# Values of layers 0 and 2 by one level of Strassen's algorithm, with the token sums of queries and keys

## Chip, cores and metric

The kernel runs on one core of one Trainium2 chip. The metric is the device time of one execution in microseconds (us). Three runs of the kernel before took 3003.57, 3005.7 and 3009.11 us; the median is 3005.7. The profile is of one more execution, of 3005.96 us, with a span of 3004.2 us from the first to the last instruction and a granted TensorE clock of 0.99.

## The reference

The input x has 128 graphs of 64 tokens with 512 features, in float32, and each graph has a boolean adjacency matrix. Four layers follow one another; each adds something to x. Before each layer the rows are normalized and negative values set to zero:

```python
h = jnp.maximum(_layernorm(x, axis=-1), 0.0)
x = x + _L0_gnn_ref(h, adj, Wq, Wk, Wv, Wo, bo)
```

Layers 0 and 2 are attention of 4 heads of 64, so Wq, Wk and Wv are 512 by 256 and Wo is 256 by 512:

```python
q = split_heads(x @ Wq); k = split_heads(x @ Wk); v = split_heads(x @ Wv)
sim = jnp.where(adjacency_mask, q @ k.T * scale, neg)
out = softmax(sim) @ v
return out @ Wo + bo
```

Layers 1 and 3 are wider forms of the same (8 heads) and are not touched by the change. Everything is float32.

## The kernel before

**Steps.** The 8192 token rows are cut into 16 blocks of 512 tokens. A step is one block in one layer: 16 steps to a layer, 64 in all, of which 32 belong to layers 0 and 2. A step loads its rows in two halves (L468, tile xin), normalizes them (DVE L433 to L442 for the statistics, with a power on POOL at L440, then ACT L449), transposes them on TensorE (L500, tile ptr; ACT copies them to the tile hT at L505), projects them to queries, keys and values, forms scores (L847, tile sc), does the softmax (DVE L858, L863, L866, L872 and L874, ACT L869, POOL L876, tile E), transposes it (L887, tile ptp), multiplies it by the values (L1006, tile po), projects by Wo and adds the residual (tile xres, loaded at L927, with the bias added by POOL at L931, stored at L972).

**Strassen products.** Queries and keys together (weights w_qk), the projection by Wo, and all projections of layers 1 and 3 are done by `winograd`: the weights A and the tokens B are split two by two, and seven products are formed instead of eight. The sums that this needs are made once for the weights (POOL, `sums_of_a`, L315), and in every step for the tokens (`sums_of_b`, tile t: by POOL at L327 from hT, by DVE at L324 from the attention's output m). A tile of weights has seven slots; a product is called here by its slot: A0, A1, A5, A4, A2, A6, A3, in the order in which they run. A0, A5, A2 and A3 go to one PSUM bank (mA), A1 to another (mB), A4 and A6 to a third (mC). A product that goes on in a bank waits for the copy of what the bank held to be read (`read` in the code): ACT copies at L552 and L572, or to the tile u at L947 for Wo, whose copies POOL adds to xres at L952. DVE adds the others (L565, L576).

**Values of layers 0 and 2.** These are done directly, by `v_proj` (L682): for each of 4 blocks of 128 tokens, 4 matmuls of 128 by 128 tokens against 256 columns of Wv, into one of the two banks that mB and mC also use (tile mmv), and one ACT copy (`evict`, L674). A float32 matmul stands in the trace as two records, called passes here.

**Order.** Nothing is scheduled by hand. Seven streams (weights, loads, layernorms, transposes, projections, fronts for scores and softmax, attentions) are Python generators; each yields what it will do next, with an assumed duration (`pe(0.432)`, `act(0.6)`) or an event to wait for. `Order.run` always takes the stream that can start earliest by these assumed times, then the one of the lower priority number, and writes its instruction. So the assumed durations settle the fixed order of instructions on each engine. [...] The SP queue issues the loads and stores of xin and xres, in order; the loads of weights go out from ACT's queue.

**Buffers that matter.** xin: 4 halves; xres: 2 halves; t: 3; hT: 2; V: 2; PSUM banks: 2 for mA, 2 shared by mB, mC, mmv and mmf, 2 for ptr and ptp, 2 for sc and po.

Of the kernel before, what the change touches and what calls it, by code (L numbers as in the profile page):

```python
# [14 lines left out]
P = 128  # L15
D = 512
N = 64
TB = 4
NC = D // P
# [163 lines left out]
def pe(us):  # L183
    return ("pe", us, 0.25)


def dve(us):
    return ("dve", us, 0.1)


def act(us):
    return ("act", us, 0.1)


def pool(us):
    return ("pool", us, 0.15)
# [7 lines left out]
def gnn_stack(ctx: ExitStack, tc: tile.TileContext, a: dict, out: bass.AP):  # L204
# [80 lines left out]

    def v_part(t):

        return t.rearrange("p a k n -> p (a k) n")[:, 0:4]

    def o_part(t):  # L290

        return t.rearrange("p a k n -> p (a k) n")[:, 4:11, None, :]

    def wo_halves(t, n):
        v = o_part(t)[:, 0:4, 0].rearrange("p (i j) n -> p i j n", i=2)
        return [(a[n][:, i * H:(i + 1) * H], v[:, i]) for i in range(2)]

    units = [("qk0", lambda t: halves(t, "Wq0", "Wk0")),
             ("vo0", lambda t: [(a["Wv0"], v_part(t))] + wo_halves(t, "Wo0")),
             ("q1", lambda t: halves(t, "Wq1")), ("k1", lambda t: halves(t, "Wk1")),  # L300
             ("v1", lambda t: halves(t, "Wv1")), ("o1", lambda t: halves(t, "Wo1")),
             ("qk2", lambda t: halves(t, "Wq2", "Wk2")),
             ("vo2", lambda t: [(a["Wv2"], v_part(t))] + wo_halves(t, "Wo2")),
             ("map3", lambda t: halves(t, "map3")), ("sem3", lambda t: []),
             ("q3", lambda t: halves(t, "q3")), ("k3", lambda t: halves(t, "k3"))]
    for key, _ in units:
        w_ready[key], w_sums[key] = od.event(), od.event()
    bo, bo_done = {}, {}

    def sums_of_a(A):  # L310

        for o, i0, i1, op in ((4, 2, 3, ALU.add), (5, 4, 0, ALU.subtract),
                              (6, 1, 5, ALU.subtract), (2, 0, 2, ALU.subtract)):
            yield pool(1.3)
            nc.gpsimd.tensor_tensor(A[:, o], A[:, i0], A[:, i1], op)  # L315

    def sums_of_b(B, T, vector=False):
# [11 lines left out]
    def weights():  # L329
        for key, parts in units:  # L330
            if key == "q1":
                yield p_ready[0, 0]
            t, w_done[key] = yield from r_w.new(f"w_{key}")
            W[key] = t
            for src, dst in parts(t):
                yield ("actq", 1.0, 10.0)
                nc.scalar.dma_start(dst, src.rearrange("(c p) o -> p c o", p=P))
            if key in ("vo0", "o1", "vo2"):
                l = int(key[-1])
                src = a[f"bo{l}"]  # L340
                bo[l], bo_done[l] = yield from r_u.new(f"bo{l}")
                yield ("actq", 0.5, 2.0)
                nc.scalar.dma_start(bo[l], bass.AP(tensor=src.tensor, offset=src.offset,
                                                   ap=[[0, P], [1, D]]))
            if key in ("q1", "k1", "v1"):
                yield from gamma_into(key)
            elif key == "o1":
                yield from v_bias()
            elif key == "sem3":
                yield from gcn_fold(t)  # L350
            w_ready[key].set()
            yield from sums_of_a(o_part(t) if key in ("vo0", "vo2") else t)
            w_sums[key].set()

    bv = const.tile([P, NC], F32, name="bv")
# [171 lines left out]

    def product(bank, A, B, tokens_out, first):

        KC = A.shape[1]  # L530
        for m in range(2):
            o = bank[:, m * H:(m + 1) * H]
            for k in range(KC):
                yield pe(0.432)
                if tokens_out:
                    l, r = B[:, k, m * P:(m + 1) * P], A[:, k, :]
                else:
                    l, r = A[:, k, m * P:(m + 1) * P], B[:, k, :]
                nc.tensor.matmul(o, l, r, start=(first and m == 0 and k == 0),  # L539
                                 stop=(k == KC - 1), skip_group_check=True)  # L540

    class Out:

# [4 lines left out]
        def first(self, i, k, p_, read, done):  # L548
            o, p3 = self.view(i, k), both(p_)
            if self.bias is None:  # L550
                yield act(0.6)
                nc.scalar.copy(o, p3)  # L552
            else:
                for m in range(2):
                    yield act(0.45)
                    nc.scalar.activation(o[:, m], p3[:, m], AF.Identity,  # L556
                                         bias=self.bias[:, 2 * i + m:2 * i + m + 1])
            read.set()
            done.set()

        def second(self, i, k, p_, after, done):
            yield after
            o = self.view(i, k)
            yield dve(0.69)
            nc.vector.tensor_add(o, both(p_), o)  # L565
            done.set()

        def add(self, i, k, p_, after, read, done):

            o, t = self.view(i, k), self.view(i, 1 - k)  # L570
            yield act(0.6)
            nc.scalar.copy(t, both(p_))  # L572
            read.set()
            yield after
            yield dve(0.7)
            nc.vector.tensor_add(o, o, t)  # L576
            done.set()

# [3 lines left out]
    def winograd(A, BT, tokens_out, out_, used, begun):  # L582

        B, T, *sums = BT

        def ev(n):
            return [od.event() for _ in range(n)]

        def first(i, k, p_):
            read, done = ev(2)  # L590
            od.spawn(out_.first(i, k, p_, read, done), 0)
            return read, done

        def second(i, k, p_, after):
            done = od.event()
            od.spawn(out_.second(i, k, p_, after, done), 0)
            return done

        def add(i, k, p_, after):
            read, done = ev(2)  # L600
            od.spawn(out_.add(i, k, p_, after, read, done), 0)
            return read, done

        p_, pe_ = yield from r_ma.new("mA")
        yield from product(p_, A[:, 0], B(0, 0), tokens_out, True)
        read, c11 = first(0, 0, p_)
        q_, qe = yield from r_mm.new("mB")
        yield from product(q_, A[:, 1], B(1, 0), tokens_out, True)
        c11 = second(0, 0, q_, c11)
        od.spawn(when([c11], qe), 0)  # L610
        yield read
        for e in sums:
            yield e
        yield from product(p_, A[:, 5], T[:, 1], tokens_out, False)
        read, u2 = first(0, 1, p_)
        r_, re_ = yield from r_mm.new("mC")
        yield from product(r_, A[:, 4], T[:, 0], tokens_out, True)
        read5, c22 = first(1, 1, r_)
        yield read
        yield from product(p_, A[:, 2], T[:, 2], tokens_out, False)  # L620
        read, c22 = add(1, 1, p_, c22)
        begun.set()
        yield read5
        yield from product(r_, A[:, 6], B(1, 1), tokens_out, False)
        c12 = second(0, 1, r_, u2)
        od.spawn(when([c12], re_), 0)
        yield read
        yield from product(p_, A[:, 3], T[:, 3], tokens_out, False)
        od.spawn(out_.alone(1, 0, p_, pe_), 0)
        od.spawn(when([c11, c12, c22, pe_], used), 0)  # L630
# [38 lines left out]
        yield begun  # L669
        return used  # L670

    def evict(o, p_, e):
        yield act(0.4)
        nc.scalar.copy(o, p_)  # L674
        e.set()

    def v_proj(inT, w, t):
        n = w.shape[2]
        p_, e = yield from r_mm.new("mmv")
        for c in range(NC):  # L680
            yield pe(0.857 * n / 512)
            nc.tensor.matmul(p_[:, 0:n], inT[:, c, t * P:(t + 1) * P], w[:, c, :],  # L682
                             start=(c == 0), stop=(c == NC - 1))
        return p_[:, 0:n], e

    st, p_ready, s_ready, p_used, with_ones = {}, {}, {}, {}, []

    def projections(steps):
        for l, s in steps:
# [4 lines left out]
            if l in (0, 2):  # L694
                yield w_ready[f"qk{l}"]
                qk, z["qk_done"] = yield from r_qk.new("qk")
                used = yield from unit(W[f"qk{l}"], (*BT, w_sums[f"qk{l}"]), False, Out(quarters(qk)))
                od.spawn(when([used], s_ready[l, s], t_done[l, s],
                              w_done[f"qk{l}"] if end else None), 0)
                z["q"], z["k"] = qk[:, 0:2, :], qk[:, 2:4, :]  # L700
                yield w_ready[f"vo{l}"]
                V, z["v_done"] = yield from r_v.new("V")
                es = [used]
                for t in range(TB):
                    p_, e = yield from v_proj(h, v_part(W[f"vo{l}"]), t)
                    od.spawn(evict(V[:, t, 0:D // 2], p_, e), 0)
                    es.append(e)
                z["v"] = V
                od.spawn(when(es, p_ready[l, s], h_done[l, s]), 0)
            elif l == 1:  # L710
                es = []
                for i, n in enumerate("qk"):
# [510 lines left out]
```

## Time and profile before

| | us busy | share of the span |
|---|---|---|
| TensorE, matmuls (PE) | 2938.9 | 98% |
| TensorE, weight loads (PEld) | 2493.5 | 83% |
| POOL | 1493.8 | 50% |
| DVE | 1744.9 | 58% |
| ACT | 1358.7 | 45% |

Layer 0 takes the stretch from 14.5 us to about 520, layer 2 that from 1437.8 to about 1950; in between and after lie layers 1 and 3. In the stretches 119.8 to 491.5 and 1522.2 to 1921.4 the steps repeat one pattern. The page's groups give, for each kind of instruction, the busy time, the mean of one in ns and, after the second bar, how long its engine stood idle just before and for whom. The timeline gives start, duration, engine, line and operation of merged neighbours, in order of time; "x16" means sixteen records, and the idle time before is in brackets. Matmul records overlap: each is the time from its start to its end, and the next starts sooner.

### The profile page before, as it was taken

The page shows a single profiled execution, that of the slowest core. Times are in us where ns is not written, and L with a number is a line of the kernel's source. Part 1 is how long each engine was busy: PE and PEld are TensorE (multiplying, and loading weights), DVE is VectorE, ACT ScalarE, POOL GpSimd, SP SyncE. Part 2 cuts the span into 40 slices and gives each one's busy share as a digit, 9 for nine tenths or more (in the row PEclk, how much of TensorE's full clock was granted, in tenths as well). Part 3 has the DMA queues.
Part 4 walks back from the last instruction along what each step waited for, and adds up shares of the span by engine and source line. Part 5 has one row for each costly group of instructions (what it writes and reads, how often), then busy time and mean ns, then how long its engine had stood idle before and what let it go on. Part 6 is the DMA issues. An engine that isn't in the chain of part 4 may idle for free.

```text
span 3004.2 us, 64290 instructions
## 1 busy us (share of the span) xinstructions
PE 2938.9 (98%) x27288; PEld 2493.5 (83%) x27288; DVE 1744.9 (58%) x2753; ACT 1358.7 (45%) x2489; POOL 1493.8 (50%) x1168
## 2 busy tenths in 40 slices
PE   8999999999999999999999999999999999999997
PEld 7888888888888888888788888887888877888876
DVE  5545566655456455445455655656666666665556
ACT  4444444544444444443444444454444444444342
POOL 6756666634434444344556656664344434344332
PEclk9999999999999999999999999999999999999998
DMA  4332323211111211212323233332223222222112
GB/s 133 106 123 87 118 98 123 83 44 66 65 44 62 69 44 52 72 51 76 114 87 123 94 109 108 113 105 62 65 75 91 76 62 62 70 79 77 54 48 62
DMA packets 162960, 244.08 MB, mean 81 GB/s; under 512 B 17393, under 2 KB 69617, under 8 KB 162673
## 3 DMA queue, kind: packets, MB, share of 16 engines
q1 hardware_dynamic: 149760, 226.56, 23.7%
q10 hardware_dynamic: 12912, 13.42, 1.4%
q8 instruction: 214, 3.51, 0.5%
q14 instruction: 74, 0.60, 0.1%
HBM read 168.60 MB, written 71.30 MB: 80 GB/s over the span
## 4 chain that ended last, share of the span: by engine, by line
PE 88%; DVE 4%; ACT 4%; DMA 2%; POOL 1%; issue 1%; SPq 0%; DVEq 0%; POOLq 0%; ACTq 0%
PE mA L539 38%; PE mC L539 19%; PE mB L539 10%; PE mmv L682 5%; PE sc L847 5%; PE ptr L500 4%; PE ptp L887 3%; PE po L1006 2%; PE po L1141 1%; ACT E L869 1%; PE mmn L796 1%; DVE sc L858 1%; DVE E L866 1%; DVE mx L863 1%; ACT m L556 1%
## 5 line engine op out<-in xcount | busy, mean ns | idle before, releaser
L931 POOL TENSOR_TENSOR xres<-xres,u 128x512 f32<-128x512 f32 x192 | 252.3, 1335 | 355.3 <-DMA xres<-x 164.9
L433 DVE BATCH_NORM_STATS2 st<-xin 128x6 f32<-128x512 f32 x320 | 215.6, 674 | 318.4 <-DMA xin<-x 256.5
L876 POOL TENSOR_TENSOR E<-E,sm 128x1024 f32<-128x1024 f32 x96 | 186.3, 1941 | 418.1 <-DVE sm L874 297.3
L952 POOL TENSOR_TENSOR xres<-xres,u 128x512 f32<-128x512 f32 x192 | 243.6, 1269 | 245.2 <-ACT u L947 239.7
L449 ACT ACTIVATE xin<-xin,rs 128x512 f32<-128x512 f32 x320 | 243.6, 808 | 108.1 <-DVE rs L442 107.9
L682 PE MATMUL mmv<-w_vo,hT 128*128 128x256 f32 x1024 | 236.2, 382 | 1.2 <-DVE xres L565 1.1
L440 POOL TENSOR_TENSOR rs<-rs,mhalf 128x2 f32<-128x2 f32 x160 | 119.1, 745 | 230.9 <-DVE rs L438 203.9
L682 PEld LDWEIGHTS mmv<-w_vo,hT 128*128 128x128 f32 x1024 | 194.5, 191 | 30.3 <-DVE xres L565 3.5
L327 POOL TENSOR_TENSOR t<-hT 128x512 f32<-128x512 f32 x128 | 185.4, 1448 | 41.0 <-ACT hT L505 41.0
L539 PE MATMUL mA<-t,w_q 128*128 128x256 f32 x768 | 188.9, 382 | 0.0
L442 DVE SCALAR_TENSOR_TENSOR rs<-mv,rs 128x2 f32<-128x2 f32 x160 | 75.2, 470 | 194.0 <-POOL rs L440 193.9
L539 PE MATMUL mA<-t,w_qk 128*128 128x256 f32 x768 | 187.8, 381 | 0.0
L505 ACT COPY hT<-ptr 128x512 f32<-128x512 f32 x256 | 151.7, 592 | 76.8 <-PE ptr L500 76.7
L539 PE MATMUL mA<-t,w_k 128*128 128x256 f32 x768 | 183.2, 381 | 2.4 <-ACT kT L556 2.3
L327 POOL TENSOR_TENSOR t<-hT,t 128x512 f32<-128x512 f32 x128 | 179.1, 1399 | 4.9
L500 PE MATMUL ptr<-ident,xin 128*128 128x128 f32 x1024 | 160.2, 280 | 13.2 <-ACT xin L449 13.2
L539 PEld LDWEIGHTS mA<-t,w_k 128*128 128x128 f32 x768 | 144.8, 190 | 25.9 <-ACT kT L556 6.0
L891 ACT COPY pt<-ptp 128x512 f32<-128x512 f32 x192 | 112.6, 587 | 110.8 <-PE ptp L887 110.8
L539 PEld LDWEIGHTS mA<-t,w_qk 128*128 128x128 f32 x768 | 144.5, 192 | 18.7
L539 PEld LDWEIGHTS mA<-t,w_q 128*128 128x128 f32 x768 | 142.3, 190 | 18.4
L872 DVE TENSOR_REDUCE sm<-E 128x16 f32<-128x1024 f32 x96 | 116.3, 1212 | 68.8 <-ACT E L869 68.8
L780 POOL TENSOR_TENSOR v<-v,gcn_row 128x512 f32<-128x512 f32 x64 | 81.3, 1302 | 150.4 <-ACT v L638 150.4
(222 smaller groups left out, 6834.5 us busy)
## 6 DMA issues: line engine op xcount, KB each, us to landing
x<-xres SPq DMA_DIRECT2D x96, 512.0 KB, 3.8
xin<-x SPq DMA_DIRECT2D x96, 512.0 KB, 3.7
xres<-x SPq DMA_DIRECT2D x64, 512.0 KB, 4.4
xin<-in_x SPq DMA_DIRECT2D x32, 512.0 KB, 3.8
xres<-in_x SPq DMA_DIRECT2D x32, 512.0 KB, 4.7
u<-rs SPq DMA_DIRECT2D x128, 128.0 KB, 3.1
xres<-x SPq DMA_DIRECT2D x256, 64.0 KB, 2.3
out<-xres SPq DMA_DIRECT2D x256, 64.0 KB, 2.1
```

The costliest lines, as they stand in the source:

```text
L327: nc.gpsimd.tensor_tensor(o, i0, i1, ALU.subtract)
L433: nc.vector.bn_stats(st, v[:, t, :])
L440: nc.gpsimd.tensor_tensor(rs[:, 0, :], rs[:, 1, :], mhalf[:, :2], ALU.pow)
L449: nc.scalar.activation(v[:, t, :], v[:, t, :], func, bias=rs[:, 2, t:t + 1], scale=rs[:, 0, t:t + 1])
L500: nc.tensor.transpose(pt[:, c, :], x[:, t, c * P:(c + 1) * P], ident)
L505: nc.scalar.copy(h[:, :, b * P:(b + 1) * P], pt)
L539: nc.tensor.matmul(o, l, r, start=(first and m == 0 and k == 0), stop=(k == KC - 1), skip_group_check=True)
L682: nc.tensor.matmul(p_[:, 0:n], inT[:, c, t * P:(t + 1) * P], w[:, c, :], start=(c == 0), stop=(c == NC - 1))
L847: nc.tensor.matmul(S[a_ * N:(a_ + 1) * N, par, col], lT[r, c, k], rT[r, c, k], start=True, stop=True)
L876: nc.gpsimd.tensor_mul(E, E, sm[:, :, None].to_broadcast([P, 16, N]))
L931: nc.gpsimd.tensor_add(xr[:, t, :], xr[:, t, :], bo[l])
L952: nc.gpsimd.tensor_add(v, v, both(u))
```

## The change

The values of layers 0 and 2 are now done by `winograd` as well, with the same token sums (tile t) that queries and keys use.

- Wv is loaded in two halves of 128 columns, into four slots of a 7-slot tile of half-width weights; Wo moves behind it in the same buffer. `sums_of_a` makes the sums of Wv first (event `wv_sums`), then those of Wo; each Wv sum is a POOL operation of 128x256, four per layer.
- `product` takes its width from the bank, `winograd` from the weights. A value product is 2 x 2 matmuls with 128 columns each and fills 128x256 of a bank. Seven make 28 matmuls, in place of 16 with 256 columns.
- The copies and additions are those of `Out`, at half the width: per step five ACT copies and three DVE additions of 128x256, in place of four ACT copies. The planner's assumed durations follow the width (`size`).
- The tile t of a step is given back when the values are done, not when queries and keys are (`t_done`).
- `evict` and `v_proj` go. Lines below move: L539 is L549, L552 is L566, L500 is L510, L931 is L933, L947 is L949.

The core of the diff:

```diff
 def product(bank, A, B, tokens_out, first):
-        KC = A.shape[1]
+        KC, n = A.shape[1], bank.shape[1] // 2
         for m in range(2):
-            o = bank[:, m * H:(m + 1) * H]
+            o = bank[:, m * n:(m + 1) * n]
             for k in range(KC):
-                yield pe(0.432)
+                yield pe(max(0.219, 0.432 * n / H))
...
-                od.spawn(when([used], s_ready[l, s], t_done[l, s],
-                              w_done[f"qk{l}"] if end else None), 0)
+                od.spawn(when([used], s_ready[l, s], w_done[f"qk{l}"] if end else None), 0)
...
-                es = [used]
-                for t in range(TB):
-                    p_, e = yield from v_proj(h, v_part(W[f"vo{l}"]), t)
-                    od.spawn(evict(V[:, t, 0:D // 2], p_, e), 0)
-                    es.append(e)
+                def vv(i, k, V=V):
+                    return V[:, 2 * k:2 * k + 2, i * P:(i + 1) * P]
+                es = [used, (yield from unit(v_part(W[f"vo{l}"]), (*BT, wv_sums[l]), True, Out(vv)))]
                 z["v"] = V
-                od.spawn(when(es, p_ready[l, s], h_done[l, s]), 0)
+                od.spawn(when(es, p_ready[l, s], t_done[l, s], h_done[l, s]), 0)
...
+            if key in ("vo0", "vo2"):
+                yield from sums_of_a(v_part(t))
+                wv_sums[int(key[-1])].set()
+                t = o_part(t)
+            yield from sums_of_a(t)
```

As the planner weighs the new durations, the order on the engines changes too. On TensorE most steps of layers 0 and 2 follow one order, 25 of 32 before and 22 after. Written by tile, with the number of matmuls or transposes (w_qk, Wo and V say whose product it is):

```
before: mA w_qk 2, ptp 4, ptr 4, mA w_qk 2, ptp 4, ptr 4, mB w_qk 2, po, ptr 4, mB w_qk 2,
        mA w_qk 2, ptr 4, mA w_qk 2, mC 4, mA 4, mC 4, mA 4 (w_qk),
        mA Wo 2, mB Wo 1, sc, mB Wo 1, mA Wo 2, V 8, mC Wo 2, mA Wo 2, mC Wo 2, mA Wo 2, V 8
after:  mA w_qk 2, ptp 4, ptr 4, mA w_qk 2, ptp 4, mB w_qk 1, ptr 4, mB w_qk 1, po, mB w_qk 1, ptr 4,
        mB w_qk 1, mA w_qk 2, ptr 4, mA w_qk 2, mC 4, mA 4, mC 4, mA 4 (w_qk),
        mA Wo 2, mB Wo 1, sc, mB Wo 1, mA Wo 2, mC Wo 2, mA V 2, mA Wo 2, mC Wo 2, mA V 2, mA Wo 2,
        mB V 4, mA V 4, mC V 4, mA V 4, mC V 4, mA V 4
```

On ACT the value copies, formerly mixed with the copies of Wo's products (u), all come after the exponential. On DVE the first addition to the values (mB) comes between the last addition to xres and the softmax's sum, and the sums of the attention's output (t from m) come after the addition of mB to qk, of which one came before it. The orders of POOL and SP in these steps are the same as before, and so is the order on all engines within layers 1 and 3.

More of the change, by code (lines that the diff above doesn't have):

```diff
@@ L286, in v_part, with wv_halves @@
     def v_part(t):
-        return t.rearrange("p a k n -> p (a k) n")[:, 0:4]
+        return t.rearrange("p a k n -> p (a k n)")[:, 0:7 * H].rearrange(
+            "p (a k n) -> p a k n", a=7, k=2)
     def o_part(t):
-        return t.rearrange("p a k n -> p (a k) n")[:, 4:11, None, :]
+        return t.rearrange("p a k n -> p (a k) n")[:, 7:14, None, :]
+    def wv_halves(t, n):
+        v = v_part(t)[:, 0:4].rearrange("p (i j) k n -> p i (j k) n", i=2)
+        return [(a[n][:, i * P:(i + 1) * P], v[:, i]) for i in range(2)]
     def wo_halves(t, n):
@@ L298, in gnn_stack @@
     units = [("qk0", lambda t: halves(t, "Wq0", "Wk0")),
-             ("vo0", lambda t: [(a["Wv0"], v_part(t))] + wo_halves(t, "Wo0")),
+             ("vo0", lambda t: wv_halves(t, "Wv0") + wo_halves(t, "Wo0")),
              ("q1", lambda t: halves(t, "Wq1")), ("k1", lambda t: halves(t, "Wk1")),
@@ L302, in gnn_stack @@
              ("qk2", lambda t: halves(t, "Wq2", "Wk2")),
-             ("vo2", lambda t: [(a["Wv2"], v_part(t))] + wo_halves(t, "Wo2")),
+             ("vo2", lambda t: wv_halves(t, "Wv2") + wo_halves(t, "Wo2")),
              ("map3", lambda t: halves(t, "map3")), ("sem3", lambda t: []),
@@ L307, in gnn_stack @@
         w_ready[key], w_sums[key] = od.event(), od.event()
+    wv_sums = {0: od.event(), 2: od.event()}
     bo, bo_done = {}, {}
@@ L313, in sums_of_a @@
                               (6, 1, 5, ALU.subtract), (2, 0, 2, ALU.subtract)):
-            yield pool(1.3)
+            yield pool(0.0026 * A.shape[2] * A.shape[3])
             nc.gpsimd.tensor_tensor(A[:, o], A[:, i0], A[:, i1], op)
@@ L351, in weights @@
             w_ready[key].set()
-            yield from sums_of_a(o_part(t) if key in ("vo0", "vo2") else t)
+            if key in ("vo0", "vo2"):
[3 more added lines that the diff above has]
+            yield from sums_of_a(t)
             w_sums[key].set()
@@ L540, in product, with size @@
                                  stop=(k == KC - 1), skip_group_check=True)
+    def size(p_, whole):
+        return 0.2 + (whole - 0.2) * p_.shape[1] / 512
     class Out:
@@ L550, in first @@
             if self.bias is None:
-                yield act(0.6)
+                yield act(size(p_, 0.6))
                 nc.scalar.copy(o, p3)
@@ L563, in second @@
             o = self.view(i, k)
-            yield dve(0.69)
+            yield dve(size(p_, 0.69))
             nc.vector.tensor_add(o, both(p_), o)
@@ L570, in add @@
             o, t = self.view(i, k), self.view(i, 1 - k)
-            yield act(0.6)
+            yield act(size(p_, 0.6))
             nc.scalar.copy(t, both(p_))
@@ L574, in add @@
             yield after
-            yield dve(0.7)
+            yield dve(size(p_, 0.7))
             nc.vector.tensor_add(o, o, t)
@@ L584, in winograd @@
         B, T, *sums = BT
+        width = 2 * A.shape[3] if tokens_out else 2 * H
         def ev(n):
@@ L604, in winograd @@
         p_, pe_ = yield from r_ma.new("mA")
+        p_ = p_[:, 0:width]
         yield from product(p_, A[:, 0], B(0, 0), tokens_out, True)
@@ L607, in winograd @@
         q_, qe = yield from r_mm.new("mB")
+        q_ = q_[:, 0:width]
         yield from product(q_, A[:, 1], B(1, 0), tokens_out, True)
@@ L616, in winograd @@
         r_, re_ = yield from r_mm.new("mC")
+        r_ = r_[:, 0:width]
         yield from product(r_, A[:, 4], T[:, 0], tokens_out, True)
@@ L670, in unit @@
         return used
[L672 to L684, printed above, removed]
     st, p_ready, s_ready, p_used, with_ones = {}, {}, {}, {}, []
```

## The prediction

> **What bounds the kernel now.** I read the page first (totals, chain, groups), then the timeline of one step, and last single groups for durations.
>
> ```profile
> span 3004.2 us, 64290 instructions
> PE 2938.9 (98%) x27288; PEld 2493.5 (83%) x27288; DVE 1744.9 (58%) x2753; ACT 1358.7 (45%) x2489; POOL 1493.8 (50%) x1168
> ...
> PE 88%; DVE 4%; ACT 4%; DMA 2%; POOL 1%; issue 1%; SPq 0%; DVEq 0%; POOLq 0%; ACTq 0%
> ...
> L682 PE MATMUL mmv<-w_vo,hT 128*128 128x256 f32 x1024 | 236.2, 382 | 1.2 <-DVE xres L565 1.1
> ```
>
> TensorE is busy for 98% of the span and is 88% of the chain. The values of layers 0 and 2 are the last row: 1024 records are 32 steps of 16 matmuls, two records (passes) to each. So a matmul less should shorten the span, unless something else closes the loop of a step. That is what the timeline of one step has to tell; this one, of layer 2, runs from its first w_qk matmul at 1613.53 to the next step's at 1644.00, 30.47 us. 25 of the 32 steps have this order, and they take 30.4 to 31.8 us.
>
> ```profile
> 1616.57 0.62 PE L500 MATMUL ptr<-ident,xin 128*128 128x128 f32 x4
> ...
> 1617.26 0.36 SPq L468 DMA_DIRECT2D xin<-x  x1
> ...
> 1617.71 0.42 SPq L927 DMA_DIRECT2D xres<-x  x1
> ...
> 1622.32 2.67 POOL L931 TENSOR_TENSOR xres<-xres,u 128x512 f32<-128x512 f32 x2 [1.79 <-issue]
> ...
> 1630.75 0.70 POOL L440 TENSOR_TENSOR rs<-rs,mhalf 128x2 f32<-128x2 f32 x1
> ...
> 1631.48 1.22 DVE L442 SCALAR_TENSOR_TENSOR rs<-mv,rs 128x2 f32<-128x2 f32 x1 [2.45 <-POOL rs L440]
> ...
> 1632.73 1.52 ACT L449 ACTIVATE xin<-xin,rs 128x512 f32<-128x512 f32 x2 [1.58 <-DVE rs L442]
> ...
> 1634.16 0.56 ACT L947 COPY u<-mA 128x512 f32<-128x512 f32 x1
> ...
> 1636.86 1.06 ACT L869 ACTIVATE E<-E 128x1024 f32<-128x1024 f32 x1 [1.18 <-DVE E L866]
> ...
> 1638.07 0.59 ACT L947 COPY u<-mC 128x512 f32<-128x512 f32 x1
> ...
> 1638.71 1.13 PE L539 MATMUL mC<-w_vo,m 128*128 128x256 f32 x4
> ```
>
> This is a loop through five engines. The second ptr transpose ends (1617.19) and frees an xin buffer. SP issues the xin load 0.07 us later, and the second xres load, next in its queue, at 1617.71. That load lands at 1622.32; the POOL works without a break (L931 twice, four token sums at L327, the power at L440) until 1631.45. DVE's L442 waits for the power, the softmax stands behind L442 in DVE's queue, the two xin activations need it, and behind them in ACT's queue wait the copy of mA (ends 1634.72), the exponential and the copy of mC (ends 1638.66). TensorE's mC product starts 0.05 us after that copy, having stood 0.31 us. In the 25 steps the xin issue is always 3.71 to 3.74 us after the step's start, and the step ends 9.27 to 9.29 us after the mA copy (9.45 in one). **TensorE is nearly full, but this loop, not TensorE alone, sets the length of a step.**
>
> [...]
>
> ```profile
> 1517.67 1.03 PE L682 MATMUL mmv<-w_vo,hT 128*128 128x256 f32 x4
> ...
> 1518.54 1.05 PE L420 MATMUL mmf<-bdw,bb 128*128 128x128 f32 x8
> ```
>
> 8 passes in 1.05 us, the last 0.275 long, so (1.05 - 0.275)/7 = 0.111 us apart; 256 columns: (1.03 - 0.38)/3 = 0.217. The weight-load records, 190 ns long, overlap. [...] L442 takes 0.16 us alone and 1.22 us where the POOL's L952 (1.27 us) runs beside it, and the DVE sums at L324 take 0.41 alone and 1.4 to 1.5 beside POOL sums.
>
> **The change, part by part.**
>
> 1. Values on TensorE. Removed per step: 16 x 2 passes x 0.2155 = 6.90 us. Added: 7 products of 4 matmuls, 56 passes x 0.1115 (between the 0.111 above and the 0.112 median of L406) = 6.24. Saved: 0.65 us a step, 21 us in 32 steps if all of it showed.
>
> 2. Handovers inside the new unit. Each product is 8 x 0.1115 = 0.89 us, and mA and mC alternate, so a bank's copy has 0.89 us. It needs 0.16 (the pass's end, 0.273 long, after the next start) + 0.04 (ACT's start after TensorE's end in the present copies) + 0.37 (128x256 copy, L674) + 0.05 = 0.62. Between the exponential and the next activations ACT holds value copies alone. The first copy stands behind the exponential, which ends 3.2 us after the mA copy; with its 0.37 it is done at +3.6, and TensorE gets there at +4.1. Cost: zero, hidden by the neighbouring product.
>
> 3. Order on TensorE, at the projection by Wo. In the old order 8 value matmuls (3.45 us) stood between Wo's second and third use of mA. Now mC's product and two value matmuls (0.86 + 0.45) do. The third use (A2) reaches its turn 2.17 us after the second's start at 1632.52, but the mA copy ends at +2.20: TensorE waits here. From the end of the copy to the next step: 0.05 + 0.10 (first pass after a wait, as at mC now) + A2 0.86 + A6 0.86 + value 0.45 + A3 0.86 + six value products 5.35 = 8.54 us, against 9.28 now. So 0.74 us is gained at this end of the loop.
>
> 4. Order on TensorE, at the transposes. In 22 of the 32 steps one mB matmul now stands ahead of the second ptr: 2 x 0.2155 = 0.43 us later. The xin load, the second xres load and all behind it move by 0.43. On DVE the first sum of the attention output (L324) now follows the mB addition instead of preceding it; it meets the POOL's L931, which it missed by half a us so far. Not shown by this trace; I bound it at 0 and 0.41 (its whole length) and take 0.2, by what a contended sum costs the POOL now (L931 1.27 and 1.45). Loop: 0.74 - 0.43 - 0.2 = **0.1 us gained per such step** (range -0.1 to 0.3). Where the xres load comes late anyway (five of the 22 steps, 9.5 to 10.4 us after the step's start instead of 8.8 to 9.3), the sums no longer meet and it is 0.3. Together 17 x 0.1 + 5 x 0.3 = 3.2 us. The orders of SP and POOL in these steps stay as they are.
>
> 5. The other ten steps (start, layer changes, last). Two keep the transposes' order: 0.74 each. One has the later ptr: 0.3. Seven are filled otherwise; I give each its 0.65. Together 6.3 us. Their waits now (added up from the distances between TensorE's starts beyond the usual ones: 18.7 us in the first 119 us, 13.8 from 1380 to 1522, of which 7.0 hang on one xres load whose place does not change) can shift by a few us either way.
>
> 6. Small things. Four more POOL weight sums per layer, 8 x 0.72 us in all, at the layer's start while TensorE does w_qk products; the t_85 sums after them wait for hT until 35.1 us, the old w_vo sums end at 29.8, so +2.9 fits. ACT: 5 copies of 256 columns for 4, 32 x 0.37 = 12 us on an engine 45% busy. DVE: 96 additions of about 0.4, 39 us at 58%. The first stands ahead of the softmax's sum, which so starts some 2 us later; E is then ready 8.1 us after the mA copy (8.5 now, where the POOL's L952 held it), and its transposes start at 9.4. The T buffer is held until the values are done, but the next writer comes 11 us later. Wv in two loads: same bytes. No cost.
>
> Sum: 3.2 + 6.3 = 9.5 us. From 3004.2 (this execution) 2994.7; the timed runs (3003.6 to 3009.1) have their median at 3005.7, so **2996 us**.
>
> **The rivals.**
>
> - The whole saving shows: the loop has more slack than I read, or the second load lands no later. Then 32 x 0.65 to 0.74 = 21 to 24 us: 2983. For: TensorE at 98%. Against: the constant 9.28 after the mA copy.
> - No change: the DVE sums cost the POOL more than 0.31 us per step, so the 22 steps lose 0.1 to 0.2 each (2 to 4 us) and the rest gives 4 to 6: 3002. [...]
> - Slower: weight loads bind. Should 56 passes in a row fall to the 190 ns of a weight-load record, a step costs 56 x 0.19 = 10.6 against 6.9, 120 us in all: 3125. It decides from 6.90/56 = 0.123 us per pass. Against: 32 one-column passes (L368, mmb) took 3.89 us in the chain's list, 0.12 each with their waits.
>
> **How the numbers follow.** Give-back with a small gain: 0.50 (2989 to 3000). Whole saving: 0.22. No change: 0.20. Slower: 0.08. The measurement can tell about 0.2%, 6 us, from no change; the likeliest case ends nearly whole under 2999.7. Faster 0.70, same 0.22, slower 0.08. The range leaves out 0.2: 2983, the whole saving's own time, to 3003.
>
> **What would show it.** The value matmuls 0.11 us apart and no wait at L549 for a v copy (step 2). A wait of about 0.6 us in layer 2 and 0.9 in layer 0 before the third mA product of Wo, for the u copy, and none before mC (step 3). The xin issue 4.16 us after the step's start instead of 3.73, the second L933 as much later, steps of 30.2 to 30.5 us (step 4). If the steps take 29.7 us, the loop was not the bound; if value passes are over 0.123 us apart, everything here is wrong.

## The result, and the profile after

The changed kernel takes 2993.9 us (four runs, 2993.4 to 2994.3); the kernel before, run beside it, 3007.4 us (3003.6 to 3009.7). The ratio is 0.9956, with a 95% interval from 0.9939 to 0.9973: 13 us less, between 8 and 18. The forecast was 2996.

The page of the kernel after, lines that answer to those shown of before:

```profile
span 2992.5 us, 66079 instructions
...
PE 2911.9 (97%) x28056; PEld 2500.4 (84%) x28056; DVE 1795.8 (60%) x2849; ACT 1378.9 (46%) x2521; POOL 1502.6 (50%) x1176
...
PE 73%; POOL 10%; ACT 4%; DMA 4%; DVE 4%; issue 3%; SPq 1%; POOLq 0%; DVEq 0%; ACTq 0%
PE mA L549 35%; PE mC L549 17%; PE mB L549 9%; POOL t L333 5%; PE sc L849 4%; PE ptr L510 3%; PE ptp L889 3%; POOL xres L933 3%; DMA xres<-x 2%; DMA xres<-in_x 2%; ACT xin L459 1%; PE po L1008 1%; PE po L1143 1%; DVE rs L452 1%; PE mmn L798 1%
```

TensorE is busy for 27 us less, but the span (of the profiled execution, 3004.2 before) is only 11.7 us shorter. The chain of waits tells where the rest is: TensorE had 88% of it and has 73% now, POOL went from 1% to 10%. Its links, POOL's token sums (t L333), the bias additions (xres L933) behind the xres loads, DVE's rs (L452) and ACT's xin (L459), are those of the loop that the prediction described. The loop was there before, but the chain hardly showed it. Now the next step starts 8.55 us after the mA copy in every one of the steps 4 to 14 and 19 to 30 (numbered as below).

TensorE's waits on the same kernel (what waited for what, us in all, times, longest):

```profile
PE mA L549 <- ACT u L949: 16.6, 23, 1.6
...
PE mA L549 <- ACT v L566: 1.5, 2, 0.9
```

The first line is the wait that the prediction placed at the third mA product of Wo, once in each of 23 steps. The second says that the handovers inside the new value unit cost nothing, but for two places in the whole run.

One step of layer 2, from 1603.64 to 1633.82 us, 30.18 us long (timeline: start, duration, engine, line, operation; idle time before and who ended it in brackets):

```profile
1607.11 0.60 PE L510 MATMUL ptr<-ident,xin 128*128 128x128 f32 x4
...
1607.79 0.36 SPq L478 DMA_DIRECT2D xin<-x  x1
...
1608.24 0.42 SPq L929 DMA_DIRECT2D xres<-x  x1
...
1612.84 2.71 POOL L933 TENSOR_TENSOR xres<-xres,u 128x512 f32<-128x512 f32 x2 [2.93 <-DMA xres<-x]
1613.05 1.38 DVE L330 TENSOR_TENSOR t<-m,t 128x256 f32<-128x256 f32 x1
1614.35 1.48 DVE L330 TENSOR_TENSOR t<-m 128x256 f32<-128x256 f32 x1
...
1621.30 0.70 POOL L450 TENSOR_TENSOR rs<-rs,mhalf 128x2 f32<-128x2 f32 x1
...
1622.03 1.21 DVE L452 SCALAR_TENSOR_TENSOR rs<-mv,rs 128x2 f32<-128x2 f32 x1 [2.44 <-POOL rs L450]
...
1623.28 1.52 ACT L459 ACTIVATE xin<-xin,rs 128x512 f32<-128x512 f32 x2 [1.99 <-DVE rs L452]
...
1624.71 0.56 ACT L949 COPY u<-mA 128x512 f32<-128x512 f32 x1
...
1625.32 1.13 PE L549 MATMUL mA<-w_vo,t 128*128 128x256 f32 x4 [0.32 <-ACT u L949]
...
1629.35 1.06 PE L549 MATMUL mA<-w_vo,t 128*128 128x128 f32 x8
```

The xin issue is 4.15 us after the step's start. POOL stands until the xres load lands, works through to the power, and the mA copy ends, behind the xin activations, at 1625.27; TensorE goes on 0.05 us later. From there to the next step 8.55 us pass. The last row shows eight value passes in 1.06 us, 0.112 us apart.

### The profile page after: what moved, and what is told of

The parts are those of the page before. It is cut to its first block, busy times and chain, and to the rows that moved or that the text cites. A ratio compares the mean times of both kernels' runs of the same rounds, so it can differ in the third digit from the quotient of the medians.

```text
span 2992.5 us, 66079 instructions
## 1 busy us (share of the span) xinstructions
PE 2911.9 (97%) x28056; PEld 2500.4 (84%) x28056; DVE 1795.8 (60%) x2849; ACT 1378.9 (46%) x2521; POOL 1502.6 (50%) x1176
## 4 chain that ended last, share of the span: by engine, by line
PE 73%; POOL 10%; ACT 4%; DMA 4%; DVE 4%; issue 3%; SPq 1%; POOLq 0%; DVEq 0%; ACTq 0%
PE mA L549 35%; PE mC L549 17%; PE mB L549 9%; POOL t L333 5%; PE sc L849 4%; PE ptr L510 3%; PE ptp L889 3%; POOL xres L933 3%; DMA xres<-x 2%; DMA xres<-in_x 2%; ACT xin L459 1%; PE po L1008 1%; PE po L1143 1%; DVE rs L452 1%; PE mmn L798 1%
## 5 line engine op out<-in xcount | busy, mean ns | idle before, releaser
L933 POOL TENSOR_TENSOR xres<-xres,u 128x512 f32<-128x512 f32 x192 | 253.0, 1338 | 335.8 <-DMA xres<-x 157.1
L459 ACT ACTIVATE xin<-xin,rs 128x512 f32<-128x512 f32 x320 | 247.1, 810 | 127.8 <-DVE rs L452 122.2
L549 PE MATMUL mA<-w_vo,t 128*128 128x128 f32 (+1 forms) x1152 | 204.1, 314 | 18.4 <-ACT u L949 16.6
L333 POOL TENSOR_TENSOR t<-hT 128x512 f32<-128x512 f32 x128 | 181.2, 1416 | 44.5 <-ACT hT L515 44.5
L549 PE MATMUL mA<-t,w_q 128*128 128x256 f32 x768 | 189.1, 382 | 0.0
L549 PE MATMUL mA<-t,w_qk 128*128 128x256 f32 x768 | 188.3, 381 | 0.6 <-POOL t L333 0.6
L549 PEld LDWEIGHTS mA<-w_vo,t 128*128 128x128 f32 x1152 | 162.6, 192 | 31.3 <-ACT u L949 22.3
L549 PE MATMUL mA<-t,w_k 128*128 128x256 f32 x768 | 182.8, 381 | 4.8 <-ACT kT L570 4.7
L333 POOL TENSOR_TENSOR t<-hT,t 128x512 f32<-128x512 f32 x128 | 180.8, 1413 | 4.9
L566 ACT COPY v<-mA 128x256 f32<-128x256 f32 (+1 forms) x144 | 63.2, 439 | 244.1 <-PE mA L549 240.8
L510 PE MATMUL ptr<-ident,xin 128*128 128x128 f32 x1024 | 158.3, 278 | 13.4 <-ACT xin L459 13.4
L549 PEld LDWEIGHTS mA<-t,w_k 128*128 128x128 f32 x768 | 144.8, 190 | 28.6 <-ACT kT L570 8.7
L549 PEld LDWEIGHTS mA<-t,w_qk 128*128 128x128 f32 x768 | 144.0, 191 | 19.2 <-POOL t L333 1.0
L549 PEld LDWEIGHTS mA<-t,w_q 128*128 128x128 f32 x768 | 142.3, 190 | 18.4
```

The source lines that it names most:

```text
L333: nc.gpsimd.tensor_tensor(o, i0, i1, ALU.subtract)
L459: nc.scalar.activation(v[:, t, :], v[:, t, :], func, bias=rs[:, 2, t:t + 1], scale=rs[:, 0, t:t + 1])
L510: nc.tensor.transpose(pt[:, c, :], x[:, t, c * P:(c + 1) * P], ident)
L933: nc.gpsimd.tensor_add(xr[:, t, :], xr[:, t, :], bo[l])
```

## The experiments

Steps of layer 0 are numbered 0 to 15 here, those of layer 2 16 to 31. Each ratio is to the kernel before, run beside the edited one on the same chip; its medians there were 3003 to 3005 us, somewhat below the 3007.4 of the four runs beside the changed kernel. The ratio of the changed kernel, 0.9956, is thus the least certain of those that follow. Two theories were to be told apart: the **loop** (second ptr, xin load, second xres load behind it on SP, POOL, power, xin activations, mA copy) sets a step's length and gave the saving back; or **TensorE's work alone** does, and the gain of 13 us is all that the products are worth.

**The place of the second ptr (e1, e2).** The edit is one number that the planner assumes. It changes nothing in the work. In the steps 4 to 14 and 19 to 30 it moves the transposes' place among the mB matmuls and, on DVE, swaps the first sum of the attention's output with the addition of mB to qk, as the change did; the two are not tried apart. The edit of the changed kernel moves one copy of hT on ACT and, in most steps of layer 0, three operations of DVE's statistics as well, and both edits shift some of the order in the first steps and in layer 1.

```diff
     def normalize(v, rs, func):
         for t in range(2):
-            yield act(0.69)
+            yield act(0.80)
```

That is e1, an edit of the kernel before. e2 is the changed kernel with 0.55 in the same place.

> The kernel before, with one of the planner's assumed durations changed (0.80 for 0.69 us of a xin activation), so that in 24 of the 32 steps one more mB matmul stands ahead of the second ptr transpose, where the changed kernel has it. The work is the same. If the loop through the second ptr, the xin load and the second xres load sets a step's length: 24 x 0.43 = 10 us longer, 3017 us (3012 to 3020), and steps of about 31.2 us. If TensorE's work alone sets it: no change, 3007 us (3004 to 3010).

> The changed kernel, with the same planner number at 0.55, so that in 23 steps the second ptr stands where it stood before the change. The work is the same. If the loop sets a step's length: 23 x 0.43 = 10 us shorter than the changed kernel, 2984 us (2980 to 2988), steps of about 30.1 us in the mean. If TensorE's work alone sets it: no change, 2994 us (2991 to 2997).

e1: 3019.5 us, ratio 1.0057 (1.0045 to 1.0069). e2: 2977.7 us, ratio 0.9915 (0.9902 to 0.9927). With the changed kernel and the kernel before these are all four cases:

| | second ptr early | one matmul later |
|---|---|---|
| values direct | 1 (before) | 1.0057 (e1) |
| values by Strassen | 0.9915 (e2) | 0.9956 (changed kernel) |

So the Strassen values are worth 0.85% (some 25 us) with the ptr early and 1.0% with it late, and the later ptr costs 0.57% and 0.41%. The change did both, and what showed is the difference. TensorE's work alone would have given the columns the same figure. In both cases the effect was larger than the 10 us expected: e1's steps 4 to 14 and 19 to 30 got 0.45 us longer each, 10.4 us in 23 steps, as expected, and the rest lies outside them; what makes it was not tried. e2's got 0.82 (layer 0) and 0.47 us (layer 2) shorter than the changed kernel's. In layer 0 more changed than the ptr's place: DVE's sums of the attention's output are through before POOL's second bias pair starts and take 0.41 to 0.43 us each, POOL needs 8.5 to 8.7 us from the start of that pair to the end of the power, and in four of the eleven steps L452 came before POOL's addition instead of beside it and took 0.16 us instead of 1.2.

**The loop cut in SP's queue, a first try (e3, e4).** `residuals` issues both xres loads, and only then yields POOL's additions to the planner.

```diff
         for k in range(2):
             xr, xe = yield from r_xres.new()
             yield load()
             nc.sync.dma_start(xr, x_of(l, s)[k * H:(k + 1) * H, :].rearrange(
                 "(t p) d -> p t d", p=P))
+            got[k] = (xr, xe)
+        for k in range(2):
+            xr = got[k][0]
             for t in range(2):
                 yield pool(1.3)
```

e3 is the kernel before with it, e4 the changed kernel with it and with 0.45 for the 0.69.

> The kernel before with both xres loads issued ahead of the POOL's bias additions, so that on SP the second xres load no longer stands behind the xin load, and the loop is cut at that place; TensorE's order is the same in 25 steps. If the loop sets a step's length: the token sums now start when hT is there instead of behind the late load, steps go from 30.8 towards 30.1 us, in all 10 to 20 us shorter: 2990 us (2987 to 2998). If TensorE's work alone sets it: no change, 3007 us.

> The changed kernel with both xres loads ahead of the bias additions and the planner number at 0.45, so that the second ptr stands at its old place in 23 steps. If the loop is what gives the saving back: TensorE is then the bound, steps of about 29.7 us, 0.9 us x 23 less than the changed kernel: 2973 us (2968 to 2980); the difference to the same edit of the kernel before is then most of the 21 us of TensorE's saving. If TensorE's work alone sets it: no change, 2994 us. If another wait takes the loop's place at once, it ends about where the early ptr alone does, 2984 us.

e3: 3037.4 us, ratio 1.0115 (1.0101 to 1.0128), slower where a gain was expected. e4: 2988.9 us, ratio 0.9956 (0.9944 to 0.9968), slower than e2 and not the 2973 expected. The load did come earlier, and the power with it (16.2 us after the step's start instead of 17.9). But the planner took the earlier power as a chance to put the xin activations ahead of a copy of queries and keys in ACT's queue. The timeline of e3 shows a step with this order:

```profile
1616.38 0.81 ACT L449 ACTIVATE xin<-xin,rs 128x512 f32<-128x512 f32 x1
1616.53 1.16 PE L847 MATMUL sc<-qk 64*64 64x64 f32 x64 [0.35 <-ACT qk L552]
...
1625.01 1.13 PE L539 MATMUL mC<-w_vo,m 128*128 128x256 f32 x4 [0.65 <-ACT u L949]
```

TensorE now stands at the scores, a product earlier than before, and again at mC. The loop was not cut but closed at another place. The edit changed two things and so decides nothing about the load; it shows that the same loop can be closed by whatever copy stands behind the xin activations.

**The loop cut in SP's queue, alone (e5, e6, e7).** The second load's instruction is written where the first one is, while the planner is still charged for it at the old place.

```diff
-        for k in range(2):
-            xr, xe = yield from r_xres.new()
-            yield load()
-            nc.sync.dma_start(xr, x_of(l, s)[k * H:(k + 1) * H, :].rearrange(
-                "(t p) d -> p t d", p=P))
+        bufs = []
+        for k in range(2):
+            bufs.append((yield from r_xres.new()))
+            if k == 0:
+                yield load()
+            nc.sync.dma_start(bufs[k][0], x_of(l, s)[k * H:(k + 1) * H, :].rearrange(
+                "(t p) d -> p t d", p=P))
+        for k in range(2):
+            xr, xe = bufs[k]
+            if k:
+                yield load()
```

TensorE, ACT, DVE and POOL keep their orders instruction by instruction; only SP's differs. e5 is the kernel before with it, e6 the changed kernel, e7 the changed kernel with e2's number as well.

> The kernel before with nothing but SP's order changed: the second xres load is issued ahead of the xin load (both right after the first xres load's place), and TensorE, ACT, DVE and POOL keep their orders instruction by instruction. If the loop closes through that load: it lands some 2 us earlier, the POOL goes from its first bias additions straight to the second ones (start at about 7.0 us of the step instead of 8.8 to 9.2), the power ends at about 16.2 instead of 17.9, and TensorE's wait ahead of mC goes: 25 steps of 30.1 us instead of 30.8, 17 us less than before, 2987 us (2983 to 2993). If it was the planner's shift of ACT's order that made the last edit of the kernel before slower, this has nothing of it. If the load's place is not what counts: no change, 3003 us.

> The changed kernel with the same edit of SP's order alone; the second ptr stays at its late place. If the loop is what gave the saving back: the wait of Wo's third mA product goes and 22 steps fall to TensorE's own 29.55 us (30.56 now): 22 us less than the changed kernel, 2971 us (2967 to 2978). If not: no change, 2993 us.

> The changed kernel with SP's order as in the last one and the second ptr at its earlier place. If the ptr's place counted only through the xin load and the xres load behind it in SP's queue, it is now worth nothing: the same time as with SP's order alone, 2971 us (2966 to 2978), steps of 29.55 us. If the ptr's place costs TensorE or ACT something of its own, its 16 us are there again: 16 us less than with SP's order alone, 2955 us.

e5: 2996.9 us, ratio 0.9975 (0.9965 to 0.9986). e6: 2981.3 us, 0.9915 (0.9900 to 0.9930). e7: 2966.9 us, 0.9875 (0.9860 to 0.9890), the fastest of all and faster than both kernels. What the cut does inside a step is seen best in one step of layer 2 of each kernel (of the first four, one whose xres load landed early); times are us after the step's start:

| | second ptr ends | second bias pair starts (POOL) | power ends | mA copy ends | next step |
|---|---|---|---|---|---|
| before | 3.65 | 8.75 | 17.87 | 21.15 | 30.43 |
| e1, ptr later | 4.07 | 9.17 | 18.36 | 21.64 | 30.92 |
| changed kernel | 4.08 | 9.21 | 18.36 | 21.63 | 30.18 |
| e2, ptr early | 3.64 | 8.72 | 17.84 | 21.12 | 29.67 |
| e5, before, cut | 3.65 | 6.88 | 16.20 | 20.64 | 30.35 |
| e6, changed, cut | 4.08 | 5.90 | 15.77 | 20.68 | 29.59 |
| e7, changed, cut, ptr early | 3.64 | 5.08 | 15.57 | 20.62 | 29.54 |

In the first four rows a shift of the ptr by 0.43 us goes through POOL and ACT to the next step, 0.49 and 0.51 us there. In the last three it goes nowhere: e6 and e7 differ by 0.05 us. And the steps are then nearly all alike, 30.35 or 30.36 us in 19 of the 23 of e5, 29.55 to 29.60 in 20 of those of e6, 29.54 or 29.55 in all 23 of e7. That is TensorE's own time. The timeline of e7 around the cut:

```profile
1613.98 0.36 SPq L931 DMA_DIRECT2D xres<-x  x1
...
1617.03 0.60 PE L510 MATMUL ptr<-ident,xin 128*128 128x128 f32 x4
1617.70 5.06 SPq L478 DMA_DIRECT2D xin<-x  x2
...
1619.07 2.50 POOL L939 TENSOR_TENSOR xres<-xres,u 128x512 f32<-128x512 f32 x2 [0.16 <-POOL xres L939]
...
1628.40 1.16 POOL L450 TENSOR_TENSOR rs<-rs,mhalf 128x2 f32<-128x2 f32 x1
1629.59 0.16 DVE L452 SCALAR_TENSOR_TENSOR rs<-mv,rs 128x2 f32<-128x2 f32 x1
...
1631.49 1.52 ACT L459 ACTIVATE xin<-xin,rs 128x512 f32<-128x512 f32 x2
...
1634.02 0.58 ACT L955 COPY u<-mA 128x512 f32<-128x512 f32 x1 [1.02 <-PE mA L549]
...
1635.13 1.03 PE L549 MATMUL mA<-w_vo,t 128*128 128x256 f32 x4
```

The xres load goes out ahead of the ptr, POOL's second pair follows the first with no load to wait for, the activations are over 1 us before the mA copy is wanted, and that copy waits for TensorE instead of TensorE for it. The third mA product of Wo starts without a wait.

Three expectations failed. e5 gained 8 us where 17 were expected: TensorE's own step is 30.35 us and not the 30.1 that was taken from the wait ahead of mC; in e5 TensorE waits for nothing in 20 of the 23 steps. In the quiet steps of the kernel before (30.43 us) the loop was thus only 0.08 us longer than TensorE's own work; in those of the changed kernel (30.18 against 29.59) it is 0.6 us longer.

e6 was to take 2971 us and took 10 more, and e7 was to equal e6, but is 14 us faster. By the totals alone that is close to the other outcome named there, that the ptr's place costs something of its own. The steps speak against it: in nearly all of them e7 does equal e6; in the two profiled executions, 20 us apart, 17 us are in three places: two steps of e6 that take 34.1 and 34.4 us, and the stretch from step 15 to step 16, 955.4 us against 947.7. So the edit of the planner's number costs e6 something against e7 through other changes of order, and not through the ptr's place in a step. In the stretch it is layer 1's product at L399, in e6 and then in e7:

```profile
561.49 0.67 PE L399 MATMUL mmb<-w_o,bb 128*128 128x256 f32 x2 [1.54 <-DVE bb L394]
564.35 4.98 PE L399 MATMUL mmb<-w_o,bb 128*128 128x256 f32 x14 [2.19 <-DMA w_o<-in_Wo]
...
550.61 3.72 PE L399 MATMUL mmb<-w_o,bb 128*128 128x256 f32 x16
```

e7 comes to it some matmuls later in its order and does not wait; 5.7 of the 7.7 us lie here. One of the two steps in e6's timeline:

```profile
210.59 1.32 POOL L333 TENSOR_TENSOR t<-hT 128x512 f32<-128x512 f32 x1
210.70 1.49 DVE L330 TENSOR_TENSOR t<-m 128x256 f32<-128x256 f32 x1
...
211.99 1.33 POOL L333 TENSOR_TENSOR t<-hT,t 128x512 f32<-128x512 f32 x1
212.11 1.48 DVE L330 TENSOR_TENSOR t<-m,t 128x256 f32<-128x256 f32 x1
212.32 1.89 PE L549 MATMUL mA<-t,w_qk 128*128 128x256 f32 x8
...
213.52 1.21 DVE L452 SCALAR_TENSOR_TENSOR rs<-mv,rs 128x2 f32<-128x2 f32 x1
...
214.77 1.52 ACT L459 ACTIVATE xin<-xin,rs 128x512 f32<-128x512 f32 x2 [3.39 <-DVE rs L452]
216.20 0.56 ACT L566 COPY qk<-mC 128x512 f32<-128x512 f32 x1
...
216.81 3.24 PE L549 MATMUL mC<-hT,w_qk 128*128 128x256 f32 x8 [2.60 <-ACT qk L566]
```

POOL's token sums come earlier than in the changed kernel and run beside DVE's, which take 1.48 and 1.49 us instead of 0.42; L452 stands behind them, the xin activations behind L452, and the copy for TensorE behind those. This place of L452 in DVE's order, in the steps 5, 6 and 14 of layer 0, is the changed kernel's own; e7 does not have it. In the changed kernel the same four sums of this step took 0.41 to 0.43 us each, while POOL was still waiting for the load (3.87 us). The wait of 2.60 us is not all: the eight passes after it take 3.24 us, where the eight of the product before took 1.89, and the granted clock was 0.66 in the 5 us from 216.0 on.

**The change in one layer alone (e8, e9).** The other layer keeps `v_proj`, its old layout of w_vo and its old sums. The core for e8; e9 has `l == 2`:

```diff
+                if l == 0:
                     es = [used, (yield from unit(v_part(W[f"vo{l}"]), (*BT, wv_sums[l]), True, Out(vv)))]
...
+                es = [used]
+                for t in range(TB):
+                    p_, e = yield from v_proj(h, v_whole(W[f"vo{l}"]), t)
+                    od.spawn(evict(V[:, t, 0:D // 2], p_, e), 0)
+                    es.append(e)
```

> The change in layer 0 alone; layer 2's values as before. In the traces of the two kernels the change gave 6.5 us in the steps 0 to 3, 4.8 us in the steps 4 to 14, and lost 6.0 us between step 15 and layer 2, where TensorE waits for Wo's load of layer 1. If the effects are local to the steps, all of that is here and nothing else: 5.3 us less than before, ratio 0.998 (0.997 to 0.9995). If the loss at layer 1's start has nothing to do with layer 0's values, it is missing here: 11 us less, 0.996.

> The change in layer 2 alone; layer 0's values as before. In the traces the change gave 4.5 us in layer 2's first three steps, 2.6 us in its twelve steady ones, and lost 0.7 us after them: 6.4 us less than before, ratio 0.998 (0.997 to 0.9995), steps of 30.5 us with a wait of about 0.8 us ahead of Wo's third mA product. If TensorE's saving showed whole where nothing of layer 0 disturbs it: 16 x 0.65 to 0.81 = 10 to 13 us less, 0.996.

e8: 2999.2 us, ratio 0.9982 (0.9975 to 0.9990), as the local reading has it. e9: 3003.4 us, ratio 0.9993 (0.9983 to 1.0002), less than expected: it lies within the range named, but the expected 0.998 is just outside the interval. In e9's profiled execution layer 2 did gain, 3.7 us in its first three steps and 2.9 in the twelve steady ones, with the wait for the u copy 12 times, 7.6 us in all; but the untouched steps 0 to 3 took 3.3 us more than in the profile before, and single executions of the kernel before differ by more, 2997 to 3013 us beside e8 and e9. A whole saving of 10 to 13 us in layer 2 is excluded. That the effects are local to the layers fits the steps, but the totals do not show it: e8 and e9 together are some 6 us faster, the changed kernel 8 to 18.

## Why the prediction held, step by step

**Values on TensorE (1)** were right: 56 passes take 6.25 us in e7's steps and the 32 old ones 6.91 us in e5's; 6.24 and 6.90 were predicted. The rival in which weight loads bind falls with it, at 0.112 us per pass against its 0.123. TensorE's own step fell somewhat more, from 30.355 to 29.544 us, because 0.15 us of small delays at other products went with it (0.08 at mC of Wo, 0.05 at its mA products). The "whole saving" rival was thus sized a little low, and it is what e7 has against e5, 1.0%.

**Handovers (2) and the order at Wo (3)** were right: two waits for a value copy in all, and the third mA product waits for the mA copy with 8.55 us left behind it (8.54 predicted). Counted by the distances between TensorE's starts the wait is 0.88 us in layer 0 and 0.83 in layer 2; 0.9 and 0.6 were predicted.

**The transposes (4)**: the place was right, xin issue at 4.15 us (4.16), and e1 shows what the later place costs together with the swap on DVE, 0.45 us a step. The term that was off is the meeting of DVE's sums with POOL's bias additions, 0.2 us in 17 steps. In the step shown above, three of DVE's four sums take 1.38 to 1.49 us beside POOL's operations, and POOL needs 9.16 us from the start of the second pair to the end of the power. But three were slowed before as well (1.49 to 1.52 us in the step of the prediction), with 9.13 us for POOL, and the sum that meets POOL's pair now is not slowed (0.41 us). Bounded from nothing to 0.41 us, the meeting should have stood at 0.03.

That does not mean that such sums cost POOL nothing. Where none of the four is slowed, POOL's stretch is 8.5 to 8.9 us in either kernel, as in this step of the changed kernel, whose load landed later; it starts at 1755.79:

```profile
1764.71 0.41 DVE L330 TENSOR_TENSOR t<-m 128x256 f32<-128x256 f32 x1
...
1765.83 0.42 DVE L330 TENSOR_TENSOR t<-m,t 128x256 f32<-128x256 f32 x1
...
1766.30 2.50 POOL L933 TENSOR_TENSOR xres<-xres,u 128x512 f32<-128x512 f32 x2 [5.17 <-issue]
...
1774.12 0.69 POOL L450 TENSOR_TENSOR rs<-rs,mhalf 128x2 f32<-128x2 f32 x1
```

Here the stretch is 8.51 us. Such steps were five of the 23 before and are nine now. The mean of the 23 steps 4 to 14 and 19 to 30, cut into its parts (us):

| | start to second pair | pair to end of power | to end of mA copy | to next step | step |
|---|---|---|---|---|---|
| before | 9.28 | 9.01 | 3.27 | 9.29 | 30.86 |
| changed kernel | 9.81 | 8.90 | 3.27 | 8.55 | 30.54 |

The last part fell by 0.73 (0.74 predicted). The first grew by 0.53 instead of 0.43, as the loads took 0.1 us longer to land in the mean; whether the change makes them land later is not shown. POOL's part fell by 0.11 us where up to 0.2 more was forecast. So the 23 steps gained 7.3 us (30.99 to 30.57 us in the mean in layer 0, 30.73 to 30.52 in layer 2) where 3.5 were forecast: some 6 us better at POOL's part, 2.3 worse at the loads. Single steps spread more than the 30.2 to 30.5 us named, from 29.96 to 31.48. The "no change" rival needed 0.31 us more of POOL in each step; that is excluded.

**The other steps (5)** gave 4.4 us where 6.0 were left for them, but not evenly: 6.6 us in steps 0 to 3 and 4.6 in 16 to 18, with 6.0 lost between step 15 and step 16 and 0.8 after layer 2. In the first of these losses TensorE comes to layer 1's `v_bias` product (L399) before Wo's load has landed: from the start of its first wait to the next product 9.55 us pass; before, from its first pass, 4.56. No kernel was made that moves this product alone. Of these only a total was forecast.

Together 11.7 us in this execution against 9.5 forecast. That the total came so near is in part luck: the steady steps gave 3.8 us more than forecast and the others 1.6 less. The mechanism was not luck: most of the saving was given back, as said, at the second ptr and through the loop.

## What to carry to other kernels

When an engine is 98% busy and yet a loop through other engines is as long as its work, work taken from the engine shows only as far as the loop gets shorter with it; look for the interval that stays constant from step to step (here 8.55 us from one copy to the next step) and ask what sets its start. A planner that writes the order from assumed durations turns any change of work into a change of order, so the order of every engine should be compared before the work is priced, and an edit meant as a test should leave all orders but one as they were: e3 and e5 make the same transfer earlier, and one is 1.2% slower and the other 0.25% faster. Here one load moved in one queue and four transposes moved by one matmul are worth more (0.8%, changed kernel to e7) than the change itself (0.44%).

## What the hardware showed unasked

Short pauses of TensorE were followed by a loss as large again: after 2.84 us of pauses, 2.9 us more went in slower work. In the changed kernel TensorE stood 1.54 us for DVE at L399 and, after two passes, 1.30 us for Wo's load; e8, whose instructions are the same up to there, stood 1.55 and 1.41 us at the same product. The timeline of the changed kernel:

```profile
560.99 0.67 PE L399 MATMUL mmb<-w_o,bb 128*128 128x256 f32 x2 [1.54 <-DVE bb L394]
562.96 6.20 PE L399 MATMUL mmb<-w_o,bb 128*128 128x256 f32 x14 [1.30 <-DMA w_o<-in_Wo]
```

and of e8:

```profile
559.43 0.67 PE L404 MATMUL mmb<-w_o,bb 128*128 128x256 f32 x2 [1.55 <-DVE bb L399]
561.50 3.29 PE L404 MATMUL mmb<-w_o,bb 128*128 128x256 f32 x14 [1.41 <-DMA w_o<-in_Wo]
```

The same fourteen passes took 6.20 us and 3.29 us. The windows of the changed kernel (stretch, its length, busy time and records of PE, PEld, DVE, ACT and POOL, granted clock, DMA share, GB/s) show the clock that went with it:

```profile
560.00:562.90 2.90, 0.67 (x2) 0.30 (x2) 2.79 (x5) 1.52 (x2) 0.88 (x1) 0.85 1.06 402
562.90:569.20 6.30, 6.24 (x15) 5.04 (x16) 4.79 (x10) 1.06 (x1) 1.45 (x1) 0.52 0.50 153
569.20:580.00 10.80, 10.80 (x55) 9.57 (x54) 4.94 (x11) 5.05 (x10) 7.72 (x8) 1.00 0.00 0
```

For 6.3 us the granted clock was 0.52; in e8 it was 1.00 in each of the windows from 557 to 570 us. That is 2.9 of the 6.0 us lost at layer 1's start. The pauses themselves were much alike: here 2.84 us of idling in 3.5, no single pause longer than 1.54 us, with the drop, and in e8 2.96 us in 3.6, without it. In the slow step of e6 a single pause of 2.60 us was followed by eight passes in 3.24 us instead of 1.89. So pauses of about this length were followed by a lower clock in two executions and not in a third; no run tests whether they are the cause, and what decides it is not shown.
